# Maxima of attention scores: one whole tile and half of another per window, instead of one and a half shared tiles

## The chip, the cores and the metric

The kernel runs on one core of one Trainium2 chip. The metric is the device time of one execution in microseconds. The kernel before was run three times: 1779.7, 1775.07 and 1778.25 us, median 1778.25 us.

A core has five engines that run side by side and meet only at semaphores: TensorE (matmuls, "PE" in the profile, its weight loads "PEld"), VectorE ("DVE"), ScalarE ("ACT"), GpSimd ("POOL") and SyncE ("SP"), which issues the DMAs here. Matmuls write to PSUM, which has eight banks of 2 KB per partition; 128x512 float32 values fill one bank. VectorE and ScalarE read PSUM and write SBUF.

## The reference, cut to what matters

```
x = x + layernorm(attention(layernorm(x)))
x = x + layernorm(ffn(layernorm(x)))

attention: q = x @ Wq  (16 heads of 16),  k, v = x @ Wk, x @ Wv  (4 heads, each used by 4 query heads)
           q, k = rope(q), rope(k)
           p = softmax(q k^T / sqrt(D))          D = 256
           out = (p v) @ Wo
ffn:       x @ (ternarized weight * alpha)^T + bias
```

The input is 8 sequences of 1024 tokens with 256 features. The softmax needs, for every query and head, the maximum of its scores over all 1024 keys before the exponentials are taken. Float32 accuracy is kept by splitting numbers into a high and a low part and stacking them along the contraction dimension.

## The kernel before, in words

**Units, blocks, windows.** The 8192 tokens form 16 units u of 512 queries (two per sequence). A unit has four blocks, j = 0 to 3, so there are 64 blocks i = 4u + j. A block computes four heads for 512 queries: for each of 8 key tiles kt, four exp tiles of 128 keys x 512 queries, 32 exp tiles in all, numbered s. Four exp tiles are a step; a unit has 32 steps. The work of a block is cut into windows: ten of three exp tiles and one of two (`windows`, L1057). The last twelve steps of the kernel are "late": their windows hold four exp tiles and no maxima.

**Two passes over the scores.** The scores are computed twice. The second pass (`exp_scores`, L659) has keys on the PSUM partitions and queries along the free dimension; ScalarE takes exp of them (L678), and the matmuls "av" (L698) multiply the result by v. The first pass (`max_scores`, L575) has queries on the partitions and keys along the free dimension, so that VectorE can reduce each row to its maximum (L621). It runs about 48 half tiles (a block and a half) ahead of the exps. Each half tile is one matmul over 512 keys; a whole maxima tile covers the 1024 keys in two halves. There are 2048 half tiles, as many as exp tiles.

**Rows of the array.** Both passes contract over 64 rows: for each head half a (0 or 1) the rows 64a to 64a+63 of the stacked queries `q_st` and keys `k_st`. Matmuls on opposite row halves run side by side on TensorE.

**How a window interleaves.** `window` (L1099) issues one exp tile, one maxima half tile, one exp tile and so on, three of each. So a whole maxima tile starts in one window and every second one is finished in the next. A tile "sm" has two PSUM banks, and the pool `ps_mx` holds two such tiles; `ps_e` holds three single banks for exp tiles (and, during the main part, for all projection and tail products, through `psum`, L186); the last bank is for av.

**The tile that crosses a window.** From block 9 on (and except for every eighth block, whose maxima need both halves alone) the crossing tile is treated differently: its first half is computed with key differences `k_df` (second 512 keys minus the first 512), ScalarE takes Relu of it into `rest` (`positive_differences`, L626, at the end of the window, after the three exps), the second half is the scores of the first 512 keys, and one fused VectorE operation adds the two and takes the maximum (L617), since max(s1, s2) = s1 + relu(s2 - s1). There are 245 such tiles. Both halves lie in the same tile "sm", in different banks.

**Maxima to shift rows.** When a block's maxima are all read, `shift_split` (L632) splits them into a high and a low part on VectorE, and two steps later `shift_rows` (L641) transposes them on TensorE ("pm"), copies them on ScalarE ("mh") and issues two DMAs (L654), one for each a, which write them as extra rows of `q_st`. The exp matmuls of that block read these rows. `parts_of_step` (L1076) tests, at the end of every step, whether a transpose is due; a window of three tiles ends a step in three windows out of four.

**Parts.** Between the exps of a window and its av matmuls `parts_of_step` also issues the projection and tail pieces of other units, at steps given by the tables `P_PARTS` and `T_PARTS` (L952 to L971). The av matmuls of a window are those of two windows earlier.

**Order.** The order on TensorE, VectorE and ScalarE is written out by hand (the program order). In the main part GpSimd and the DMA issues on SP are ordered by the framework's scheduler. Every engine works strictly in its order. Whole tiles are tracked for dependences.

**The start.** Before the first exp there are ten steps of maxima alone, four half tiles each (`start_step`, L1082).

Of the kernel before, what the change touches and what calls it, by code (L numbers as in the profile page):

```python
# [8 lines left out]
F32 = mybir.dt.float32  # L9
# [20 lines left out]
def kernel(  # L30
# [49 lines left out]
    avp = ctx.enter_context(tc.tile_pool(name="avp", bufs=5))  # L80
    tailp = ctx.enter_context(tc.tile_pool(name="tailp", bufs=1))
    dram = ctx.enter_context(tc.tile_pool(name="dram", bufs=3, space=DRAM))
    ps_mx = ctx.enter_context(tc.tile_pool(name="ps_mx", bufs=2, space=PSUM))
    ps_e = ctx.enter_context(tc.tile_pool(name="ps_e", bufs=3, space=PSUM))
    ps_av = ctx.enter_context(tc.tile_pool(name="ps_av", bufs=1, space=PSUM))

# [99 lines left out]
    def psum(shape, name, dtype=F32):  # L186
        if spare[0]:
            spare[0] += 1
            if spare[0] % 5 < 2:
                return ps_mx.tile(shape, dtype, tag="sm", name=name)  # L190
        return ps_e.tile(shape, dtype, tag="se", name=name)


# [114 lines left out]
    class Project:  # L308
# [3 lines left out]
        def __init__(self, u, eng):  # L312
            self.u, self.eng = u, eng
            self.b, self.half = divmod(u, UPB)
            self.xt, self.sc, self.hl = {}, {}, {}
            self.q_rot = None
            if u not in (1, 2):
                xn = qkp.tile([P, UT, D], F32, tag="xn", name=f"xn_{u}", bufs=2)
                xs = qkp.tile([P, 2, UT, D], F32R, tag="hl", name=f"xs_{u}")
                self.xn = [xn[:, 2 * p : 2 * p + 2, :] for p in range(2)]  # L320
                self.xs = [[xs[:, l, 2 * p : 2 * p + 2, :] for l in range(2)] for p in range(2)]
            else:
                self.xn = [
                    tailp.tile([P, 2, D], F32, tag=f"xn{p}", name=f"xn_{u}_{p}") for p in range(2)
                ]
                self.xs = [
                    [ep.tile([P, 2, D], F32R, tag="e", name=f"xs_{u}_{p}_{l}") for l in range(2)]
                    for p in range(2)
                ]
# [238 lines left out]
    def block_queries(i, r2=slice(None)):  # L568

        u, j = divmod(i, G)  # L570
        if u < NU - 1:
            return q_st[u % 2][:, j, r2, :]
        return q_st[u % 2][:, :, r2, j * P : (j + 1) * P]

    def max_scores(v, end):  # L575

        i, k = divmod(v // 2, 2 * NK)  # L580
        u, part = i // G, v % 2
        if i == 0:
            a, ch, t, r2 = 1 - part, k // NK, k // 2 % UT, k % 2
        else:
            a, ch, t, r2 = 1 - k % 2, part, k // 4, k // 2 % 2
        queries = block_queries(i, r2)
        queries = queries[:, t * P : (t + 1) * P] if u < NU - 1 else queries[:, t]
        keys = k_st[(u // UPB) % 2][:, :, ch * 512 : (ch + 1) * 512]
        if part == 0:
            sm[0] = ps_mx.tile([P, 2, 512], F32, tag="sm", name=f"sm_{i}_{k}")  # L590
            if k == 0:
                mx[i] = small.tile([P, 2, UT, 2], F32, tag="mx", name=f"mx_{i}")
            if k == 0 and i == 0:
                mx["half"] = small.tile([P, 2, 2, UT, 2], F32, tag="mx0", name="mx_half", bufs=1)
            sm["rest"] = None
            if v + 1 == end and u >= UPB and i % (UPB * G) > 0:
                sm["rest"] = work.tile([P, 512], F32, tag="rest", name=f"rest_{i}_{k}")
                keys = k_df
        elif sm["rest"] is not None:
            keys = k_st[(u // UPB) % 2][:, :, :512]  # L600
        rows = slice(64 * a, 64 * a + 64)
        nc.tensor.matmul(  # L602
            sm[0][:, part, :],
            queries[rows],
            keys[rows, r2],
            start=True,
            stop=True,
        )
        if part == 0:
            return  # L610
        if i == 0:
            nc.vector.tensor_reduce(mx["half"][:, ch, ::-1, t, r2], sm[0], AX.X, ALU.max)
            if k == 2 * NK - 1:
                nc.vector.tensor_tensor(mx[0], mx["half"][:, 0], mx["half"][:, 1], ALU.max)
        elif sm["rest"] is not None:
            rest, m = sm["rest"], mx[i][:, a, t, r2 : r2 + 1]
            nc.vector.tensor_tensor_reduce(  # L617
                rest, sm[0][:, 1, :], rest, 1.0, LEAST, ALU.add, ALU.max, m
            )
        else:  # L620
            nc.vector.tensor_reduce(mx[i][:, a, t, r2 : r2 + 1], sm[0], AX.XY, ALU.max)  # L621
        if k == 2 * NK - 1:
            shift_split(i)
            due.append((v // 4 + (1 if i < 2 else 2), i))

    def positive_differences(v):  # L626
        if v % 2 and sm["rest"] is not None:
            nc.scalar.activation(sm["rest"], sm[0][:, 0, :], AF.Relu)  # L628

    sm, mhl, shifts = {}, {}, {}  # L630

    def shift_split(i):  # L632

        m = mx.pop(i)
        hl = mhl[i] = small.tile([P, 2, 2, 2 * UT], F32R, tag="mhl", name=f"mhl_{i}")
        order = "(r t)" if i // G < NU - 1 else "(t r)"
        hi, lo = (hl[:, :, l].rearrange(f"p a {order} -> p a t r", r=2) for l in range(2))
        nc.vector.tensor_copy(hi, m)  # L638
        split_lo(nc.vector, lo, m, hi)
# [19 lines left out]
    def exp_scores(n, r2, a, sc):  # L659
        i, kt = divmod(n, NK)  # L660
        queries = block_queries(i, r2)
        rows = slice(64 * a, 64 * a + 64)
        nc.tensor.matmul(  # L663
            sc if len(queries.shape) == 2 else sc.rearrange("p (j t) -> p j t", j=G),
            k_st[(i // G // UPB) % 2][rows, r2, kt * P : (kt + 1) * P],
            queries[rows],
            start=True,
            stop=True,
        )

    def exp_one(s):

        n, (a, r2) = s // 4, divmod(s % 4, 2)
        i, kt = divmod(n, NK)
        e = es[n, r2, a] = ep.tile([P, UQ], F32, tag="e", name=f"e_{i}_{kt}_{r2}_{a}")
        sc = ps_e.tile([P, 512], F32, tag="se", name=f"se_{i}_{kt}_{r2}_{a}")
        exp_scores(n, r2, a, sc)
        nc.scalar.activation(e, sc, AF.Exp, scale=1.0 / D**0.5)  # L678

    def exp_two(n, r2):  # L680

        i, kt = divmod(n, NK)
        sc = ps_mx.tile([P, 2, 512], F32, tag="sm", name=f"se_{i}_{kt}_{r2}")
        for a in range(2):
            exp_scores(n, r2, a, sc[:, a, :])
        for a in range(2):
            e = es[n, r2, a] = ep.tile([P, UQ], F32, tag="e", name=f"e_{i}_{kt}_{r2}_{a}")
            nc.scalar.activation(e, sc[:, a, :], AF.Exp, scale=1.0 / D**0.5)

    def av_piece(i, first, end):  # L690

# [30 lines left out]
    class Tail:  # L722
# [9 lines left out]
        def new(self, what, p):  # L732
            shape, dtype = ([P, 2, 2, D], F32R) if what == "hl" else ([P, 2, D], F32)
            return tailp.tile(shape, dtype, tag=f"{what}{p}", name=f"{what}_{self.u}_{p}")
# [7 lines left out]
        def tiles(self, p):  # L742
            return slice(self.width * p, self.width * (p + 1))
# [306 lines left out]
    for k, *p in L_PARTS:  # L1050
        at(SPU * (NU - 1) + k, part, tails, NU - 1, *p)

    def maxima_by(s):

        return s + 4 * START + 2 * sum(s >= k for k in (28, 36, 52, 68))

    def windows():  # L1057


# [11 lines left out]
                yield i, s, size, s >= ends  # L1071
                s += size

    maxima = [0]

    def parts_of_step(n):  # L1076
        if due and due[0][0] <= maxima_by(4 * n + 4) // 4 - 1:
            shift_rows(due.pop(0)[1])
        for f, args in todo.pop(n, ()):
            f(*args)  # L1080

    def start_step(n):  # L1082
        for _ in range(4):
            max_scores(maxima[0], None)
            maxima[0] += 1
        parts_of_step(n)

    behind, done = [], []
# [10 lines left out]
    def window(i, s, size, late):  # L1099
        if done:  # L1100
            av_out(done.pop())
        if late:
            for r2 in range(2):
                exp_two(s // 4, r2)
        else:
            end = min(maxima_by(s + size), 4 * NSTEP)
            for q in range(max(size, end - maxima[0])):
                if q < size:
                    exp_one(s + q)
                if maxima[0] < end:  # L1110
                    max_scores(maxima[0], end)
                    maxima[0] += 1
            positive_differences(maxima[0])
        behind.append((i, s, size))
        for n in range(s // 4, (s + size) // 4):
            parts_of_step(n)
        av_windows(1 if late else 2)
# [59 lines left out]
    with tc.manual_schedule(engines={E.PE, E.DVE, E.Activation}):  # L1177
        for w in work_left:
            window(*w)
        av_windows(0)  # L1180
        av_out(NU * G - 1)
        assert not todo and not due
    spare[0] = 1
    with tc.manual_schedule(engines={E.PE, E.DVE, E.Activation, E.Pool}):
        last = tails[NU - 1]
# [67 lines left out]
```

## Time and profile before

| what | value |
|---|---|
| median of three runs | 1778.25 us |
| profiled execution | 1778.75 us |
| span of the profiled execution | 1777.0 us |
| mean granted TensorE clock | 0.988 |
| TensorE busy | 1635.8 us, 92% of the span |
| ScalarE busy | 1391.9 us, 78% |
| VectorE busy | 1272.2 us, 72% |
| GpSimd busy | 846.1 us, 48% |

The costliest groups, with the mean duration of one instruction:

| line, engine | what | count | mean ns |
|---|---|---|---|
| L678 ACT | exp of a tile of scores, 128x512 | 2000 | 604 |
| L621 DVE | maximum over a whole tile, 128x1024 to 128x1 | 763 | 1219 |
| L612 DVE | the same for block 0, 128x1024 to 128x2 | 16 | 1220 |
| L617 DVE | fused add and maximum, 128x512 | 245 | 692 |
| L628 ACT | Relu of the differences, 128x512 | 245 | 626 |
| L663 PE | scores for exp | 2048 | 434 |
| L602 PE | scores for maxima | 1803 + 245 | 454, 458 |

How to read it. "Busy" counts the time in which an instruction was running; matmuls overlap, so their durations are longer than the distance from one start to the next. The chain of waits follows the execution back from its end: at each instruction to what released it, or to the instruction before it on its engine. A row of the waits view names who waited, for whom, the total in us, how often, and the longest. In the timeline each row is a start, a duration, the engine, the line, and what it writes and reads; a bracket gives the idle time before it and what ended it.

### The profile page before, as it was taken

To read this page: it belongs to the slowest core of one execution; us is meant where nothing else is said; L and a number is where in the kernel's file an instruction comes from. 1 tells how busy PE (TensorE), PEld (TensorE's weight loads), DVE (VectorE), ACT (ScalarE), POOL (GpSimd) and SP (SyncE) were. 2 spreads that over 40 slices of the span, in tenths; PEclk is the share of its full clock that TensorE was granted. 3 is DMA by queue.
4 is the path that set the end of the run, shared out by engine and by line. 5 is a ranking of instruction groups with operands and counts; after the bars stand their busy time and mean duration, and the time that the engine had idled before them with its cause. 6 is when DMAs were issued, how large, how long until landed. Compare 5 with 4: busy or idle time off the path is not lost.

```text
span 1777.0 us, 36663 instructions
## 1 busy us (share of the span) xinstructions
PE 1635.8 (92%) x14200; PEld 843.9 (47%) x14200; DVE 1272.2 (72%) x1997; ACT 1391.9 (78%) x2724; POOL 846.1 (48%) x1259
## 2 busy tenths in 40 slices
PE   7999899989999999999999999999999999999997
PEld 5544354444544445454444445444454444444444
DVE  6777787666776677767777677766777667777764
ACT  4667678788887878878788787888878788888885
POOL 5543374373744536364373745537373452323354
PEclk8899999999999999999999999999999999999999
DMA  4151425142251513315141241513325141231100
GB/s 125 52 102 42 94 67 108 44 91 60 81 97 42 102 46 86 79 58 99 53 99 46 82 93 42 107 46 84 65 62 101 38 97 41 47 68 32 39 13 25
DMA packets 91790, 122.41 MB, mean 69 GB/s; under 512 B 12872, under 2 KB 55176, under 8 KB 91496
## 3 DMA queue, kind: packets, MB, share of 16 engines
q1 hardware_dynamic: 91616, 120.06, 29.2%
q8 instruction: 112, 1.84, 0.5%
q14 instruction: 62, 0.51, 0.1%
HBM read 71.27 MB, written 47.71 MB: 67 GB/s over the span
## 4 chain that ended last, share of the span: by engine, by line
PE 52%; ACT 28%; DVE 8%; POOL 4%; DMA 4%; issue 3%; SPq 1%; ACTq 0%; POOLq 0%
ACT e L678 21%; PE av L698 17%; PE se L663 15%; PE sm L602 9%; ACT rest L628 5%; DVE mx L621 4%; PE pa L286 3%; PE pq L286 2%; PE pf L286 2%; PE pkv L286 1%; ACT avsb L711 1%; PE pt_xt L270 1%; DVE rest L617 1%; PE pt_ot L270 1%; DVE mhl L638 1%
## 5 line engine op out<-in xcount | busy, mean ns | idle before, releaser
L678 ACT ACTIVATE e<-se 128x512 f32<-128x512 f32 x2000 | 1082.1, 604 | 254.6 <-PE sm L602 206.4
L621 DVE TENSOR_REDUCE mx<-sm 128x1 f32<-128x1024 f32 x763 | 916.4, 1219 | 167.7 <-PE sm L602 137.2
L663 PE MATMUL se<-q_st,k_st 64*128 64x512 f32 x2048 | 704.3, 434 | 9.9 <-DMA q_st<-mh 8.8
L602 PE MATMUL sm<-k_st,q_st 64*128 64x512 f32 x1803 | 578.6, 454 | 72.9 <-ACT rest L628 64.8
L698 PE MATMUL av<-e,v_aug 128*32 128x256 f32 (+3 forms) x8096 | 591.4, 392 | 0.0
L663 PEld LDWEIGHTS se<-q_st,k_st 64*128 64x128 f32 x2048 | 342.3, 186 | 378.6 <-ACT e L678 247.0
L617 DVE CUSTOM_DVE_ANT_0 rest<-sm,rest 128x512 f32<-128x512 f32 x245 | 169.5, 692 | 285.9 <-PE sm L602 281.1
L602 PEld LDWEIGHTS sm<-k_st,q_st 64*128 64x128 f32 x1803 | 244.8, 187 | 158.6 <-ACT rest L628 122.0
L698 PEld LDWEIGHTS av<-e,v_aug 128*32 128x32 f32 x8096 | 184.4, 109 | 190.1 <-issue 141.2
L244 POOL TENSOR_SCALAR lnsc<-mv 128x2 f32<-128x2 f32 (+1 forms) x134 | 26.1, 195 | 479.6 <-DVE mv L242 474.7
L628 ACT ACTIVATE rest<-sm 128x512 f32<-128x512 f32 x245 | 153.5, 626 | 0.9 <-PE sm L602 0.9
L602 PE MATMUL sm<-k_df,q_st 64*128 64x512 f32 x245 | 112.2, 458 | 9.2 <-DVE mx L621 7.4
L772 POOL TENSOR_TENSOR xn<-xn,a 128x512 f32<-128x512 f32 x30 | 38.4, 1281 | 139.3 <-DMA a<-d_rec 139.2
L833 POOL TENSOR_TENSOR a<-a,bias_bc 128x512 f32<-128x512 f32 x30 | 39.0, 1301 | 125.6 <-ACT a L832 125.6
L245 POOL TENSOR_TENSOR lnsc<-lnsc,mhalf 128x2 f32<-128x2 f32 (+1 forms) x134 | 92.7, 692 | 0.9
L165 POOL TENSOR_TENSOR hl<-xn,hl 128x512 fp32r<-128x512 f32 x60 | 76.4, 1284 | 0.5
L602 PEld LDWEIGHTS sm<-k_df,q_st 64*128 64x128 f32 x245 | 45.0, 184 | 47.4 <-DVE mx L621 40.2
L256 POOL TENSOR_SCALAR xn<-x,lnsc 128x256 f32<-128x256 f32 x116 | 64.3, 562 | 3.4
L300 POOL TENSOR_TENSOR t<-q_rot,sin_q_sb 128x512 f32<-128x512 f32 x31 | 40.0, 1290 | 15.6 <-ACT q_rot L452 15.6
L240 DVE BATCH_NORM_STATS2 bnst<-a 128x6 f32<-128x256 f32 x120 | 44.6, 413 | 3.7 <-POOL a L833 3.7
L286 PE MATMUL pa<-woh,hl 128*128 128x256 f32 x240 | 46.1, 294 | 0.4 <-ACT e L678 0.2
L240 DVE BATCH_NORM_STATS2 bnst<-x 128x6 f32<-128x256 f32 x124 | 46.0, 413 | 0.7 <-DMA x<-in_L_attn_x 0.7
(168 smaller groups left out, 1469.6 us busy)
## 6 DMA issues: line engine op xcount, KB each, us to landing
q_st<-dq SPq DMA_DIRECT2D x90, 256.0 KB
dq<-hlq SPq DMA_DIRECT2D x60, 256.0 KB
d_av<-avsb SPq DMA_DIRECT2D x60, 256.0 KB
x<-in_L_attn_x SPq DMA_DIRECT2D x15, 512.0 KB
xn<-d_av SPq DMA_DIRECT2D x30, 256.0 KB
a<-d_rec SPq DMA_DIRECT2D x30, 256.0 KB
xr<-in_L_attn_x SPq DMA_DIRECT2D x15, 512.0 KB
out_x<-a SPq DMA_DIRECT2D x30, 256.0 KB
```

Source lines behind the costliest of these rows:

```text
L165: eng.tensor_tensor(lo, src, hi.bitcast(F32), ALU.subtract)
L240: nc.vector.bn_stats(st[:, t, :], src[:, t, :])
L245: nc.gpsimd.tensor_tensor(sc[:, 1, :], sc[:, 1, :], mhalf[:, :n], ALU.pow)
L256: eng.tensor_scalar(dst[:, t, :], src[:, t, :], sc[:, 0, t : t + 1] if eng is nc.gpsimd else mv[:, t, 0:1], sc[:, 1, t : t + 1], ALU.add i ...
L286: nc.tensor.matmul(out, chunk(left[i], c), chunk(right[j], c), start=(k == 0), stop=(k == len(steps) - 1),)
L602: nc.tensor.matmul(sm[0][:, part, :], queries[rows], keys[rows, r2], start=True, stop=True,)
L617: nc.vector.tensor_tensor_reduce(rest, sm[0][:, 1, :], rest, 1.0, LEAST, ALU.add, ALU.max, m)
L621: nc.vector.tensor_reduce(mx[i][:, a, t, r2 : r2 + 1], sm[0], AX.XY, ALU.max)
L628: nc.scalar.activation(sm["rest"], sm[0][:, 0, :], AF.Relu)
L663: nc.tensor.matmul(sc if len(queries.shape) == 2 else sc.rearrange("p (j t) -> p j t", j=G), k_st[(i // G // UPB) % 2][rows, r2, kt * P : ...
L678: nc.scalar.activation(e, sc, AF.Exp, scale=1.0 / D**0.5)
L698: nc.tensor.matmul(av_ps[0][32 * r : 32 * r + 32, lo:hi], va[:, kt, r, :], es[i * NK + kt, r // 2, r % 2][:, lo:hi], start=(kt == 0 and lo ...
```

## The change

The crossing tile disappears. A window of three now holds one whole tile (two matmuls, one head half a) and one half of another. The pool `ps_mx` keeps its four banks, but as one tile "two" of two banks and a ring of two single banks "one". The whole tile goes through tag "two" with a single buffer, each half through tag "one". Late windows and spare tiles use the same tags.

Halves always belong to head half 0. First and second halves alternate from window to window; where differences apply, the first half is the one with `k_df` and the Relu, the second the one with the fused operation, as before. In the other blocks (block 0 to 8 and then every eighth) each half is reduced by itself, every reduction writes one maximum per half, and `shift_split` takes the larger of the two. Whole tiles belong to the head half opposite to the window's last exp tile, and the order of heads among the four exp tiles of a key tile now follows a pattern of three. The first exp tile of a block is now one of head half 1. The reads are issued after all matmuls of the window: the whole tile's reduction first, then the half's Relu, fused operation or reduction.

A shift transpose is due 8 half tiles after its block's maxima are read (4 for blocks 0 and 1), counted in half tiles issued. Four places in the first blocks (`AHEAD`) issue two more half tiles each, which brings the lead to 48. The two-exp window of a block holds a whole tile and no half.

```diff
-    ps_mx = ctx.enter_context(tc.tile_pool(name="ps_mx", bufs=2, space=PSUM))
+    ps_mx = ctx.enter_context(tc.tile_pool(name="ps_mx", bufs=1, space=PSUM))
...
+        def whole(self, a):
+            i, halves = self.next_tile(a)
+            tile = ps_mx.tile([P, 2, 512], F32, tag="two", name=f"sm_{i}_{a}_{halves[0][1]}")
+            self.done += 2
...
+        def half(self):
+            first = self.open is None
+            if first:
+                self.open = (*self.next_tile(0), None)
+            i, halves, rest = self.open
...
+            tile = ps_mx.tile([P, 512], F32, tag="one", name=f"sh_{i}_{t}_{r2}_{ch}", bufs=2)
+            self.done += 1
...
+                if not self.differences(i):
+                    m = mx[i][:, ch, 0, t, r2 : r2 + 1]
+                    nc.vector.tensor_reduce(m, tile, AX.X, ALU.max)
+                elif first:
+                    nc.scalar.activation(rest, tile, AF.Relu)
+                else:
+                    m = mx[i][:, 0, t, r2 : r2 + 1]
+                    nc.vector.tensor_tensor_reduce(
+                        rest, tile, rest, 1.0, LEAST, ALU.add, ALU.max, m
+                    )
...
+        def read(self, i):
+            self.unread[i] -= 1
+            if self.unread[i] == 0:
+                shift_split(i)
+                due.append((self.done + (4 if i < 2 else 8), i))
...
+    def exp_order(s):
+        kt = s // 4 % NK
+        if s < 4 * NK and kt >= 2:
+            kt -= 2
+        a = ((1, 0, 0, 1), (0, 0, 1, 1), (1, 1, 0, 0))[kt % 3]
+        q = s % 4
+        return a[q], a[:q].count(a[q])
...
     def parts_of_step(n):
-        if due and due[0][0] <= maxima_by(4 * n + 4) // 4 - 1:
+        if due and due[0][0] <= maxima.done + behind_maxima[0]:
             shift_rows(due.pop(0)[1])
...
+            work, reads = [], []
+            if size == 3 or maxima.done + 1 == 4 * NSTEP:
+                work, read = maxima.half()
+                reads.append(read)
+            if size > 1:
+                two, read = maxima.whole(1 - exp_order(s + size - 1)[0])
+                work += two
+                reads.insert(0, read)
+            for q in range(size):
+                exp_one(s + q)
+                if q < len(work):
+                    work[q]()
+            for read in reads:
+                read()
```

## The prediction

> **What bounds the kernel now.** Read the page's chain of waits first, because engine shares mislead here: TensorE is 92% busy, yet its part of the chain is 52%.
>
> ```profile
> PE 52%; ACT 28%; DVE 8%; POOL 4%; DMA 4%; issue 3%; SPq 1%; ACTq 0%; POOLq 0%
> ACT e L678 21%; PE av L698 17%; PE se L663 15%; PE sm L602 9%; ACT rest L628 5%; DVE mx L621 4%; PE pa L286 3%; PE pq L286 2%; PE pf L286 2%; PE pkv L286 1%; ACT avsb L711 1%; PE pt_xt L270 1%; DVE rest L617 1%; PE pt_ot L270 1%; DVE mhl L638 1%
> ```
>
> The chain alternates between TensorE and ScalarE, so a dependence between them sets the pace. Who waits for whom names it:
>
> ```profile
> PEld sm L602 <- ACT rest L628: 122.0, 183, 0.8
> PE sm L602 <- ACT rest L628: 64.8, 178, 0.5
> PE sm L602 <- DVE mx L621: 13.9, 35, 1.3
> PE se L663 <- DMA q_st<-mh: 8.8, 5, 5.4
> ```
>
> Columns: total us, times, longest. The second half of a shared maxima tile is not written until the Relu has read the first half, although they lie in different banks. The timeline shows two windows (block 8) and this wait:
>
> ```profile
> 283.20 1.58 ACT L678 ACTIVATE e<-se 128x512 f32<-128x512 f32 x3 [0.47 <-PE sm L602]
> 283.23 0.39 PE L602 MATMUL sm<-k_df,q_st 64*128 64x512 f32 x1
> 283.46 1.22 DVE L621 TENSOR_REDUCE mx<-sm 128x1 f32<-128x1024 f32 x1 [0.49 <-PE sm L602]
> 283.56 0.86 PE L698 MATMUL av<-e,v_aug 128*32 128x128 f32 x16
> 284.35 0.49 PE L663 MATMUL se<-q_st,k_st 64*128 64x512 f32 x1
> 284.65 0.62 ACT L628 ACTIVATE rest<-sm 128x512 f32<-128x512 f32 x1
> 285.12 0.63 ACT L678 ACTIVATE e<-se 128x512 f32<-128x512 f32 x1
> 285.32 0.50 PE L602 MATMUL sm<-k_st,q_st 64*128 64x512 f32 x2 [0.48 <-ACT rest L628]
> 286.21 0.64 PE L698 MATMUL av<-e,v_aug 128*32 128x256 f32 x8
> ```
>
> The window starting at 282.66 takes 1.68 us. The next starts at 284.35 with one exp matmul, then stands until 285.32, because the Relu started at 284.65 after three exps: 2.43 us. The pair takes 4.11.
>
> TensorE's own window, from the same starts: pairs of matmuls in opposite row halves at 0, 0.335 and 0.57, the av matmuls 0.32 after the third pair, the next window 0.785 later: 1.675 us. The Relu's loop costs 0.75 a pair.
>
> **The change, part by part.** *Matmuls:* 2048 exp, 2048 maxima and the av matmuls remain. Within a window the new order of heads still puts opposite row halves next to each other: e1 h0 | e0 w1 | e0 w1, or e1 h0 | e1 w0 | e1 w0. Nothing gained or lost.
>
> *Removed:* the wait for the Relu, since each half now has its own bank and its ring of two is read long before reuse.
>
> *Added:* the only whole tile ("two", one buffer) cannot be written before VectorE has read the last window's. From rows: second matmul of the tile to start of the reduction 0.46 (283.00 to 283.46); reduction 1.225; its end to the released matmul 0.054 (in each such wait); after that standstill the tile's second matmul comes 0.335 later (460.68 to 461.02). Loop: 0.46+1.225+0.054+0.335 = 2.08 us. TensorE alone goes from one tile to the next in 0.32+0.785+0.335 = 1.44, against 1.74: it stands 0.30 and restarts 0.10 slower. Behind the waiting matmul stand, in program order, the window's third exp matmul, its parts and the av matmuls; ScalarE waits for the exp. So a plain pair goes from 4.11 to 4.16: **the loop through ScalarE is exchanged for one through VectorE of the same length.**
>
> The gain is in windows that carry projection or tail matmuls: these stand between the tile's end and the next tile and cover the reduction. Such a window costs 1.675 plus its part: 0.51 (four transposes), 1.15 (eight matmuls) or 1.62 (twelve). In the kernel before the part comes on top of the Relu's wait in every second window.
>
> Here a rule speaks against the change. The Trainium skill, "Perfetto Trace Analysis", section Optimizing Tensor Performance, says that independent matmul groups should rotate through different PSUM banks so that one's evacuation overlaps the next's matmuls; one whole tile doesn't rotate. If nothing covered it, each of some 640 windows would pay 1.74 instead of 0.40, +860 us. The row decides: exp, half and av matmuls use other banks and cover 1.44 of it. I take 0.40.
>
> *ScalarE* keeps its exps and 245 Relus (640 halves in windows make as many split tiles). Seven activations a pair at 0.477 from start to start are 3.34 of 4.16: not the bound. A part's PSUM tile waits for the first exp of its window, as now: 0.29 where the window before had a part too, and 0.2 in each block's third window, which starts with the avsb copy.
>
> *VectorE:* in the 15 blocks without differences, some 160 single-bank reductions replace 80 double ones. No row shows one: between 610 ns (half of 1219) and 692 (the fused op on 512). By the latter it adds 80 x (2x692-1219) = 13 us, beside TensorE; I take nothing on the path, at most 13. Layer-norm statistics (0.96 a batch) delay the next reduction: after a window with a fused op, 0.46+1.14+0.62+0.96 = 3.18 against 2.08+0.46, so 0.66, once in a j=0 block; elsewhere they follow a window with a part.
>
> *Moved:* the shift rows. A block's maxima are complete in its sixth window, as before, but the transpose pm (due 8 halves later, tested only where a step ends) goes from the eighth to the tenth window, two of 2.08 later. Then mh is copied and SP issues two DMAs. Rows: issues 0.72 apart; landing to first exp 2.13 after issue (361.24 to 363.37 below). In addition the first exp is now head half 1, which needs the second DMA. From the tenth window's last maxima matmul: pm at 0.32, ScalarE free for mh at 1.02, first issue 1.29, second 2.01, usable 4.14. The next block's first exp would start at 2.08+0.32+0.785 = 3.18 plus the eleventh window's part. With no part (j=0) it is late by 0.96, of which 0.56 counts, since the standstill for the reduction lies in it. Parts of 1.15 and 1.62 leave 0.2 and 0.7 us spare. SP's queue is the danger; its timeline at the end of block 10:
>
> ```profile
> 356.90 4.30 SPq L493 DMA_DIRECT2D k_st<-dk  x6
> 361.24 1.41 SPq L654 DMA_DIRECT2D q_st<-mh  x2
> 362.75 2.34 SPq L437 DMA_DIRECT2D dkd<-dkds  x4
> ```
>
> In j=2 blocks of odd units the shift DMAs stood behind the key stacking, whose dk comes from POOL and DRAM: issued 25.1 to 26.4 us into the block in four of them, 24.7 and 24.1 in two. The block gets shorter, the DMA chain doesn't: by the sum below the landing is 0.2 to 2.7 late, 1.6 on average, where now it is just in time. If SP orders them otherwise this goes to nothing; if they fall behind the next four DMAs (2.34 us), to 5.
>
> **The sum,** by blocks of 32 exps (ten windows of three, one of two, four kinds j=0 to 3), against starts read from the trace (282.66, 306.71, 334.86, 363.37, 391.00):
>
> - j=0: 8x2.08 + (2.19+0.2) + (2.19+0.29) + 2.19 + 0.66 + 0.56 = 24.9; now 24.0. 14 blocks: +12.
> - j=1: 7x2.08 + 2.19 + (3.30+0.29) + (2.19+0.29) + 3.30 = 26.1; now 28.0 in eleven, 26.6 to 28.5 in three. -24.
> - j=2: 8x2.08 + (3.30+0.2) + 3.30 + 3.30 = 26.7; now 26.4 in five even units; 27.5 to 28.8 in six odd ones, +1.6 for the landing there. +2.
> - j=3: 5x2.08 + 3x2.19 + (2.19+0.29+0.2) + (2.83+0.29) + 2.83 = 25.6; now 27.6 in six, 26.3 in the five that hold no Relu for most of the block, 26.8 and 27.7 in two. -18.
> - Start and the first eight blocks: no Relu there to save, VectorE on the chain (its pairs of reductions take 2.37); between -5 and +15, taken as +5 (DMA landings and single reductions).
> - The last twelve steps and the last tail: same banks, same instructions, 0.
>
> Sum -23 against the profiled span of 1777.0, that is 1754.0, or 1755.75 with the 1.75 that lies around the span (run 1778.75). The runs' median is 1778.25, 0.5 below; from it: **1755 us.**
>
> **Rivals.** (1) *The full exchange:* shift rows land in time everywhere and statistics find cover, so 14x(0.56+0.66) + 10 of late landings go: 1755-27 = 1728. For it: SP often idles for over ten us. Against: four odd units have no slack now.
>
> (2) *Nothing gained:* parts' gains are eaten by VectorE, if half of the other seven batches of statistics per unit pay 0.44 more: 15x7x0.5x0.44 = +23, 1778. Against: they come after windows with large parts.
>
> (3) *Slower:* the shift DMAs, now last before use, get queued behind other SP work. Place: first exp of every block. Price: one more group of 1.6 us (three q_st<-dq and a fill) before them makes the four transitions late by 1.6, 0.9, 0.9 and 1.4 more (1.6 less the spares of 0.7, 0.7, 0.2): 4.8 a unit, x14 = 67 us, giving 1822; at the units' ends and the odd units alone (14x1.4 + 6x1.6 + 14x0.56) some +37, 1792. It decides from a mean of 0.4 us per block (23 us over 56 blocks). For it: SP is the one queue not ordered by hand, and the next unit's queries come free in the tenth window. Against: before, those DMAs came after the shift rows.
>
> (4) *The change doesn't do what it says:* TensorE still waits for the Relu through another dependence: 0.75 on top of some of the 2.08 loops. The halves are separate tiles; little chance, and it would be slower too.
>
> **How the numbers follow.** Forecast 0.47 (own range 1740 to 1771), full exchange 0.13, nothing gained 0.12, SP queue 0.25, Relu still waited for 0.03. Some 5 us (0.3%) is what a measurement tells from none. Faster: 0.45 of the forecast's 0.47 and all of (1), 0.58; same: 0.02 and 0.08 of (2), 0.10; the rest, with 0.04 of (2), slower, 0.32. The range leaves out 0.1 at each end: 1726 to 1800.
>
> **What would show it.** Right: TensorE's wait for ACT rest is gone; sm waits for DVE mx some 400 times; plain windows start 2.08 apart; windows with twelve matmuls take about 3.3 to 3.6; se waits for q_st<-mh at some twenty block starts, up to 2.7 us. Wrong: q_st<-mh waits at most block starts, plain windows far from 2.08, or gaps at the reduction beyond 0.7 in many windows.

## The result: 5% slower, and the profile after

The changed kernel takes 1865.56 us (median of four runs, 1864.16 to 1867.1) beside 1776.66 us for the kernel before (now a median of four runs). The ratio is 1.0499, with a 95% interval of 1.048 to 1.0517. The experiments below have their own runs of the kernel before beside them (medians 1778.51 to 1780.23 us), and their ratios are to these. One run of `due3` took 2260.02 us at a granted clock of 0.698 and is left out of its median. The profiled execution has a span of 1863.6 us at a mean granted TensorE clock of 0.957; before it was 1777.0 us at 0.988.

The chain of waits of the kernel after, by engine and by line:

```profile
PE 54%; ACT 12%; DMA 12%; DVE 11%; POOL 6%; SPq 3%; issue 2%; POOLq 0%; ACTq 0%; DVEq 0%
PE av L772 17%; PE se L719 14%; PE sm L620 11%; ACT e L747 9%; DMA q_st<-mh 7%; DVE mx L637 5%; PE pa L286 3%; PE pkv L286 2%; SPq L710 1%; PE pt_xt L270 1%; ACT rest L672 1%; DMA k_rot<-d_k 1%; DVE mx L642 1%; PE pq L286 1%; DVE bnst L240 1%
```

ScalarE's share has fallen from 28% to 12%, as it should when the Relu's loop goes. DMA has tripled, from 4% to 12%, and 7% of the chain is q_st<-mh alone: the shift rows. TensorE's longest waits in the kernel after (total us, times, longest us):

```profile
PE se L719 <- DMA q_st<-mh: 115.8, 40, 7.3
PE sm L620 <- DVE mx L637: 7.7, 19, 0.9
```

The 64.8 us for the Relu are gone. In their place stands what was fourth with 8.8 us: the first exp of a block waits for its shift rows. The plain windows do what was forecast. TensorE's timeline in block 12, the first exp of four windows and one wait for the whole tile:

```profile
431.82 0.50 PE L719 MATMUL se<-q_st,k_st 64*128 64x512 f32 x1
...
433.49 0.50 PE L719 MATMUL se<-q_st,k_st 64*128 64x512 f32 x1
...
435.58 0.50 PE L719 MATMUL se<-q_st,k_st 64*128 64x512 f32 x1
...
437.63 0.50 PE L719 MATMUL se<-q_st,k_st 64*128 64x512 f32 x1
...
438.78 0.49 PE L620 MATMUL sm<-k_st,q_st 64*128 64x512 f32 x1 [0.42 <-DVE mx L637]
```

The distances are 1.67, 2.09 and 2.05 us: a plain window behind a plain one settles at the 2.08 worked out from the reduction's loop, after a first one that finds the tile free.

### The profile page after: what moved, and what is told of

The parts are those of the page before. It is cut to its first block, busy times and chain, and to the rows that moved or that the text cites. A ratio compares the mean times of both kernels' runs of the same rounds, so it can differ in the third digit from the quotient of the medians.

```text
span 1863.6 us, 36435 instructions
## 1 busy us (share of the span) xinstructions
PE 1679.1 (90%) x14200; PEld 836.1 (45%) x14200; DVE 1281.3 (69%) x2091; ACT 1374.8 (74%) x2724; POOL 845.2 (45%) x1259
## 3 DMA queue, kind: packets, MB, share of 16 engines
q8 instruction: 112, 1.84, 0.4%
## 4 chain that ended last, share of the span: by engine, by line
PE 54%; ACT 12%; DMA 12%; DVE 11%; POOL 6%; SPq 3%; issue 2%; POOLq 0%; ACTq 0%; DVEq 0%
PE av L772 17%; PE se L719 14%; PE sm L620 11%; ACT e L747 9%; DMA q_st<-mh 7%; DVE mx L637 5%; PE pa L286 3%; PE pkv L286 2%; SPq L710 1%; PE pt_xt L270 1%; ACT rest L672 1%; DMA k_rot<-d_k 1%; DVE mx L642 1%; PE pq L286 1%; DVE bnst L240 1%
## 5 line engine op out<-in xcount | busy, mean ns | idle before, releaser
L637 DVE TENSOR_REDUCE mx<-sm 128x1 f32<-128x1024 f32 x539 | 659.1, 1223 | 445.6 <-PE se L719 247.8
L719 PE MATMUL se<-q_st,k_st 64*128 64x512 f32 x2048 | 759.9, 465 | 115.8 <-DMA q_st<-mh 115.8
L620 PE MATMUL sm<-k_st,q_st 64*128 64x512 f32 x1398 | 504.9, 440 | 16.7 <-DVE mx L637 7.7
L244 POOL TENSOR_SCALAR lnsc<-mv 128x2 f32<-128x2 f32 (+1 forms) x134 | 25.6, 191 | 552.3 <-DVE mv L242 547.4
L642 DVE TENSOR_REDUCE mx<-sm 128x2 f32<-128x1024 f32 x160 | 195.8, 1224 | 92.5 <-PE sm L620 47.8
L620 PE MATMUL sh<-k_st,q_st 64*128 64x512 f32 x405 | 209.7, 521 | 4.3 <-DVE mx L670 4.0
L675 DVE CUSTOM_DVE_ANT_0 rest<-sh,rest 128x512 f32<-128x512 f32 x245 | 166.6, 680 | 0.1
L672 ACT ACTIVATE rest<-sh 128x512 f32<-128x512 f32 x245 | 155.1, 633 | 0.0
L620 PE MATMUL sh<-k_df,q_st 64*128 64x512 f32 x245 | 126.0, 514 | 0.0
L670 DVE TENSOR_REDUCE mx<-sh 128x1 f32<-128x512 f32 x160 | 107.8, 680 | 0.0
L620 PEld LDWEIGHTS sh<-k_st,q_st 64*128 64x128 f32 x405 | 77.6, 193 | 10.1 <-DVE mx L670 8.2
```

Of the source, the lines that this page charges most:

```text
L620: nc.tensor.matmul(dst, queries[rows], keys[rows, r2], start=True, stop=True)
L637: nc.vector.tensor_reduce(mx[i][:, a, t, r2 : r2 + 1], tile, AX.XY, ALU.max)
L642: nc.vector.tensor_reduce(dst, tile, AX.X, ALU.max)
L670: nc.vector.tensor_reduce(m, tile, AX.X, ALU.max)
L672: nc.scalar.activation(rest, tile, AF.Relu)
L675: nc.vector.tensor_tensor_reduce(rest, tile, rest, 1.0, LEAST, ALU.add, ALU.max, m)
```

## The experiments

**Theory:** the new windows gain what the sum says, and the loss comes from the shift rows alone: the transpose pm, two windows later, makes them land after TensorE is ready. **Rivals:** the new windows themselves are slow; or the granted clock is the cause and not a consequence.

### Moving the transpose alone, in both kernels

`due6` is the kernel after with the transpose due two half tiles earlier, which puts pm back in the eighth window. `before_late` is the kernel before with pm moved to the tenth. `due3` moves pm to the seventh window.

```diff
-                due.append((self.done + (4 if i < 2 else 8), i))
+                due.append((self.done + (4 if i < 2 else 6), i))
```

> The changed kernel with the shift transpose due 6 instead of 8 half tiles after a block's maxima, which puts it back into the eighth window (the tenth in the changed kernel). Theory L (the shift rows land too late, and TensorE then runs at half clock for a while): the wait of se for q_st<-mh falls from 115.8 us to under 20, the granted clock returns to 0.98 or more, and the time is 1725 to 1750 us, faster than before. Rival V (the single whole tile and its loop through VectorE is what costs): the waits fall, but the time stays above 1800 us.

```diff
-            due.append((v // 4 + (1 if i < 2 else 2), i))
+            due.append((v // 4 + (1 if i < 2 else 3), i))
```

> The kernel before with the shift transpose one step later, which puts it into the tenth window of a block; nothing else of the change. Theory L: most of the loss appears here without the change, se waits 70 to 110 us for q_st<-mh, the clock falls to about 0.96, 1830 to 1880 us. Rival V: within 10 us of 1777.

`due3` differs from `due6` only in its 3 in place of 6.

> As due6, but the transpose due 3 half tiles after the maxima, so in the seventh window. Theory L: no wait is left that earliness can remove (what remains stands in SP's queue behind the key stacking), within 6 us of due6 (1749). If lateness still costs in due6: 8 us or more below it.

Measured: `due6` 1749.32 us, ratio 0.9834 (0.9802 to 0.9866); `before_late` 1875.05, ratio 1.0537 (1.0484 to 1.0589); `due3` 1747.19, ratio 0.9816 (0.9794 to 0.9839). TensorE's wait for the shift rows in `due6`:

```profile
PE se L719 <- DMA q_st<-mh: 10.0, 5, 5.5
```

and TensorE's two longest waits in `before_late`:

```profile
PE se L663 <- DMA q_st<-mh: 100.2, 39, 5.3
PE sm L602 <- ACT rest L628: 51.9, 154, 0.5
```

The late transpose makes the old kernel some 97 us slower, and without it the new one is 29 us faster than the old (both beside 1778.51). So the windows are not slow. The place of one small transpose decides the sign. One window earlier still, in `due3`, adds nothing that the runs can tell: 2 us, with runs of one kernel up to 7 us apart. In the eighth window it is early enough.

### Which part of the late landing costs what

The landing isn't late for one reason. In the kernel after, from block 8 on, the waits at the starts of blocks are of three kinds: 3.1 to 3.9 us at the start of a unit (2 to 14), 1.9 to 2.3 us after a unit's first block (units 2 to 10, then 0.5 to 0.9), and 5.0 to 7.3 us ahead of the fourth block of every second unit (2 to 12). Elsewhere there is none, but for two of 0.8 near the end.

The first kind, the start of unit 3. The kernel after, the chain of waits in order of time (start us, us, what):

```profile
411.74 0.09 ACT mh L703
411.83 0.02 issue
411.84 0.67 SPq L710
412.51 0.04 issue
412.56 5.05 DMA q_st<-mh
417.61 0.14 issue
417.75 0.47 PE se L719
```

and its SP queue there, in the timeline:

```profile
410.55 0.78 SPq L559 DMA_DIRECT2D q_st<-dq  x2
411.84 1.37 SPq L710 DMA_DIRECT2D q_st<-mh  x2
413.25 1.91 SPq L559 DMA_DIRECT2D q_st<-dq  x4
```

mh ends at 411.83 and the DMA is issued at 411.84, so SP isn't late at all. The transfer of 8 KB takes 5.05 us because it runs among six 256 KB stackings (two issued ahead of it, four behind) of the next unit's queries.

The third kind, block 11. The kernel after, SP's timeline:

```profile
375.35 3.83 SPq L493 DMA_DIRECT2D k_st<-dk  x6
379.22 1.09 SPq L437 DMA_DIRECT2D dkd<-dkds  x2
382.47 0.78 SPq L493 DMA_DIRECT2D k_df<-dkd  x2
383.35 1.09 SPq L437 DMA_DIRECT2D dkd<-dkds  x2
384.54 1.40 SPq L710 DMA_DIRECT2D q_st<-mh  x2
```

Here mh was ready at 376.6. SP issues it at 384.54: the scheduler has put the writes and first reads of the key differences ahead, and SP stands from 380.3 to 382.5 until a write has landed. The transfer itself is then as short as in the prediction, 1.97 us in the chain.

Four kernels separate the first and the third. `a1first` issues the DMA that the first exp needs ahead of the other one. `actq` issues both on ScalarE's queue, so that they no longer stand in SP's order. `shift_first` holds the stacking of the next queries behind the shift DMAs of the block concerned. `shift_first2` holds the writes of the key differences behind theirs as well.

```diff
-        for a in range(2):
+        for a in (1, 0):
```

> The changed kernel with the shift DMA of head half 1, which the first exp needs, issued ahead of that of head half 0 (0.72 us from issue to issue). Theory L: each of some 40 waits gets up to 0.7 us shorter, 1830 to 1850 us. Rival O (the loss is the order of heads, whose first exp needs the second DMA): the waits go and the time is under 1790.

```diff
-            shifts[i] = nc.sync.dma_start(out=dst, in_=mh[n * a : n * a + n, :]).ins
+            shifts[i] = nc.scalar.dma_start(out=dst, in_=mh[n * a : n * a + n, :]).ins
```

> The changed kernel with the two shift DMAs issued on ScalarE's queue instead of SP's. If the SP queue's order is what delays them: the 5 to 7 us waits in the third block of odd units fall to about 1, the 3 to 4 us waits between units stay where the transfer itself is slow (5.05 us instead of 2.0 beside the next unit's queries), 1810 to 1840 us. If it is the lateness alone whatever the queue: waits of odd units stay, within 10 us of 1865.

```diff
-        at(SPU * (u - 1) + 1, stack_queries, u)
+        at(SPU * (u - 1) + 1, behind_shift, G * (u - 1), stack_queries, u)
```

> The changed kernel, with the next unit's query DMAs (q_st<-dq, six of 256 KB) held back until the shift DMAs of the block that starts have been issued. If the shift transfer is slow because it shares the DMA engines with them (5.05 us instead of 2.0 between units): the waits of 3.1 to 3.9 us at the start of each unit fall under 0.7, the others stay, 1805 to 1825 us. If those waits are the lateness of the transpose alone: they stay, 1855 us or more.

```diff
-            for l in range(2):
-                for e in range(2):
-                    nc.sync.dma_start(out=dst[l, e], in_=hl[:, l, e, :].bitcast(F32))
+            def issue():
+                for l in range(2):
+                    for e in range(2):
+                        nc.sync.dma_start(out=dst[l, e], in_=hl[:, l, e, :].bitcast(F32))
+
+            if tag == "dkd" and self.u > 3:
+                behind_shift(G * (self.u - 2) - 1, issue)
+            else:
+                issue()
```

> The kernel of the run that put the stacking of the next queries behind the shift DMAs, and now the four writes dkd<-dkds of the key differences are held behind the shift DMAs of the block in question too, so that these stand on SP right behind the key stacking and before the writes and the reads k_df<-dkd that wait for them. Theory (the 5 to 8 us at the fourth block of every second unit are SP's queue: the shift rows stand behind writes and reads of the key differences): these six waits fall to 1 to 3 us, those after the first blocks of units (about 2.3 us) stay, TensorE waits for q_st<-mh some 40 to 50 us instead of 75, and the time falls from 1814 to 1780 to 1797. Rival (the key stacking alone, which comes late from POOL and DRAM, holds the queue): the waits stay above 4 us and the time within 6 us of 1814. Whatever is left over the 1749 of the kernel with the earlier transpose is then the transpose's own place and the transfers beside which it runs.

| kernel | us, median | ratio to before (95%) | wait for shift rows, us (times) | unit starts | after first blocks | fourth block of every second unit |
|---|---|---|---|---|---|---|
| after | 1865.56 | 1.0499 (1.048 to 1.0517) | 115.8 (40) | 3.1 to 3.9 | 1.9 to 2.3 | 5.0 to 7.3 |
| a1first | 1858.10 | 1.0443 (1.0409 to 1.0477) | 101.5 (44) | 2.4 to 3.3 | 1.7 to 2.1 | 4.8 to 7.6 |
| actq | 1923.15 | 1.0813 (1.0775 to 1.085) | 164.9 (40) | 8.8 to 10.0 | 2.1 to 2.5 | 0.9 to 3.2 |
| shift_first | 1814.05 | 1.0187 (1.0165 to 1.0209) | 75.4 (26) | 0 | 1.9 to 2.8 | 5.0 to 7.9 |
| shift_first2 | 1772.33 | 0.9948 (0.9933 to 0.9962) | 43.5 (23) | 0 | 1.8 to 2.7 | 0 to 2.8 |
| due6 | 1749.32 | 0.9834 (0.9802 to 0.9866) | 10.0 (5) | 0 | 0 | 0 to 1.7 |

The last three columns are the lengths of single waits in us, for the units just named (units 2 to 10 for the second kind).

`a1first` gained 7 us where 15 and more were expected, a miss. Where the shift transfer is alone, in the last three units, the wait did fall by the issue distance, from 0.8 or 0.9 us to 0.2. At unit starts it fell by 0.6 on average, after first blocks (units 2 to 10) by 0.2, at the fourth blocks not at all. And of the 14 us less waiting half came back: the first two windows of blocks 8 to 61 take 7.4 us more, at a mean clock of 0.952.

`actq` is the larger miss, and the more telling one. Its chain at a unit's start:

```profile
418.37 0.27 ACT mh L703
418.64 0.02 issue
418.66 0.65 ACTq L710
419.31 0.04 issue
419.35 11.57 DMA q_st<-mh
430.92 0.14 issue
431.06 0.76 PE se L719
```

The DMA is issued at once on its own queue, and it takes 11.57 us, with three of the stackings put in motion by SP at 417.37, ahead of it, and three more at 419.42, while it runs. A queue of its own did not help this transfer beside the large ones. The Trainium skill ("DMA: Bandwidth & Descriptors", section Issuing engines are not separate DMA queues) says that DMAs of all issuing engines run on the same 16 DMA engines and interleave there. At the fourth blocks, where SP's order was the cause, the same edit took the waits from 5.0 to 7.3 down to 0.9 to 3.2. What is left there is not SP's order: in all six, ScalarE issues the DMA 1.7 to 4.1 us after mh is ready, released by the landing of a key stacking (k_st<-dk).

In `shift_first` the waits at unit starts go to nothing (51 us less), in `shift_first2` those at the fourth blocks shrink too (42 us less). The first came in where the theory put it; the second is 8 us below the range given, with its waits as expected. In `shift_first2`, the same stretch of SP's timeline:

```profile
371.61 3.53 SPq L499 DMA_DIRECT2D k_st<-dk  x6
375.18 1.41 SPq L716 DMA_DIRECT2D q_st<-mh  x2
376.69 2.34 SPq L438 DMA_DIRECT2D dkd<-dkds  x4
```

The shift rows stand right behind the key stacking, as they do in `due6`. With pm still in the tenth window, order on SP alone turns 5% slower into 0.5% faster. What is left to `due6`, 23 us, lies where blocks begin: over blocks 8 to 61 the last windows, in which the waits fall, hold 15.7 us more, and the first two 7.3.

### What a standstill costs beyond itself

In block 11 of the kernel after the wait is not over when the rows land. Busy time of PE, PEld, DVE, ACT and POOL by stretch, then the granted clock, DMA share and GB/s:

```profile
380.00:387.30 7.30, 0.13 (x4) 0.00 (x0) 0.00 (x0) 0.00 (x0) 7.14 (x10) 0.82 0.22 60
387.30:388.00 0.70, 0.62 (x4) 0.58 (x6) 0.00 (x0) 0.00 (x0) 0.70 (x2) 0.50 0.35 82
...
390.00:391.00 1.00, 1.00 (x12) 0.50 (x6) 0.33 (x1) 0.25 (x1) 1.00 (x3) 0.50 0.27 100
391.00:392.00 1.00, 0.88 (x7) 0.38 (x3) 0.08 (x1) 0.77 (x2) 1.00 (x2) 0.75 0.00 0
392.00:394.00 2.00, 1.95 (x18) 1.04 (x18) 1.75 (x3) 2.00 (x5) 2.00 (x2) 1.00 0.00 0
```

TensorE comes back at half clock and has it until about 391.5; its first window takes 3.02 us instead of 1.68. To price this, `warm_wait` adds matmuls of its own ahead of the first exp of a block, into that exp's PSUM tile, which the exp then overwrites: 22 of them at the fourth blocks, 12 at unit starts, 6 after first blocks.

```diff
+        if s % (4 * NK) == 0 and 8 <= s // (4 * NK) < 62:
+            j = s // (4 * NK) % (2 * G)
+            for _ in range({0: 12, 4: 12, 1: 6, 5: 6, 3: 22}.get(j, 0)):
+                nc.tensor.matmul(sc, ident_r, k_st[n // NK // G // UPB % 2][:, 0, :512], start=True, stop=True)
```

> The changed kernel with dummy matmuls of 128x512 written into the PSUM tile of a block's first exp, where TensorE waits for the shift rows anyway (12 at the start of a unit, 6 at its second block, 22 at the fourth block of every second unit[...]). If the half clock after a wait comes from TensorE standing idle: windows 0 and 1 of the blocks lose some 24 us in sum, the granted clock returns to 0.98, 1835 to 1850 us, with the same waits for the DMA. If the clock falls for another reason: within 6 us of 1865.

Measured: 1851.83 us, ratio 1.0398 (1.0374 to 1.0421), 2 us above what was expected, and a mean clock of 0.984 instead of 0.957. TensorE at the start of block 11:

```profile
376.30 5.40 PE L744 MATMUL se<-k_st,ident_r 128*128 128x512 f32 x22
382.05 0.50 PE L719 MATMUL se<-q_st,k_st 64*128 64x512 f32 x1 [0.35 <-DMA q_st<-mh]
```

The rows still land late (5.75 us after the added matmuls begin, against a stop of 7.25), but the exp now runs at full clock (0.50 us against 0.76). Over blocks 8 to 61 the first two windows of all blocks get shorter by 27.8 us in sum, while the last windows, with the added matmuls, take 8.6 us more and the windows between 5.5 more. Half clock is a consequence of the waits and costs time of its own. Of the 111 us that lie between the kernel after and `due6` in these blocks, the first two windows hold 24.

### A version that beats both

`due6` still pays the single whole tile: 2.05 in a plain window behind a plain one. `split_ring` puts every half tile into a bank of its own, one ring of four; a whole tile is then two single-bank reductions, and the Relu or fused operation is issued right behind the window's first pair. The maxima are kept per half in all blocks.

```diff
-            tile = ps_mx.tile([P, 2, 512], F32, tag="two", name=f"sm_{i}_{a}_{halves[0][1]}")
+            tiles = [
+                ps_mx.tile([P, 512], F32, tag="one", name=f"sm_{i}_{a}_{h}_{self.done}", bufs=4)
+                for h in range(2)
+            ]
...
-                due.append((self.done + (4 if i < 2 else 8), i))
+                due.append((self.done + (4 if i < 2 else 6), i))
...
+                if q == 0 and early:
+                    early[0]()
```

> As due6, but every maxima half tile has a bank of its own in one ring of four; a whole tile is two single-bank reductions (0.60 us from start to start instead of 1.14 for both at once), and the Relu or the fused operation of the half is issued ahead of the rest. If the loop through VectorE (single whole tile) is what holds plain windows at 2.05 us: they fall to 1.7 to 1.8 and the time to 1665 to 1700 us. If VectorE itself becomes the bound: 1730 to 1760 us.

Measured: 1702.44 us (1697.6 to 1704.15), ratio 0.9553 (0.9531 to 0.9574), 2 us above the range of the theory that the single whole tile was the bound, and far from its rival's 1730 to 1760. Half of the plain windows take 1.70 us or less (1.86 in `due6`), a quarter still 2.18 or more. Page of `split_ring`, the cost of it on VectorE:

```profile
PE 1589.0 (93%) x14200; PEld 785.8 (46%) x14200; DVE 1365.9 (80%) x2888; ACT 1367.9 (80%) x2724; POOL 848.2 (50%) x1259
...
L639 DVE TENSOR_REDUCE mx<-sm 128x1 f32<-128x512 f32 x1398 | 892.6, 683 | 134.7 <-PE se L716 95.4
```

Two reductions of 683 ns replace one of 1223, so VectorE has 83 us more to do than in `due6` (1282.7), and the kernel is 47 us faster all the same: VectorE's load was not the bound. The ring and the earlier reads were not tried apart.

## Why the prediction was wrong

**Right: the windows.** The wait for the Relu is gone. Ahead of a whole tile TensorE (PE and PEld together) waits for the reduction 407 times (some 400 forecast). Plain windows behind plain ones settle at 2.05 to 2.09 us (2.08 forecast). Without its landing terms, 14 x 0.56 and 6 x 1.6, the sum over the blocks was -45 us (12 - 24 + 2 - 18, less 17.4); `due6` has -40.8 over blocks 8 to 61. By kind of block the mean lengths in `due6` are 23.4, 26.7, 26.3 and 26.1 us, against 24.3 (24.9 less the 0.56), 26.1, 26.7 and 25.6 forecast. The start and the first eight blocks were taken as +5; `due6` has +12.7, inside the -5 to +15.

The kinds miss by up to 0.9 us in both directions, so that the total, 4 us off, is closer than its parts: in that much it is luck. One placement in the sum is wrong without harm. A part stands behind its own window's tile, so it covers the reduction for the next window, not for its own. In `due6` a three-exp window with twelve matmuls takes at least 3.64 us, loop and part (2.05 + 1.62), where the sum had 3.3 to 3.6, and the plain window behind a part takes 1.69 on average, where it had 2.08. Each part covers one reduction either way.

**Wrong: the landing, under "Moved".** Some twenty waits for the shift rows, of at most 2.7 us, were forecast; there were 40, of up to 7.3. The prediction priced the landing at 2.13 us from issue to first exp everywhere, and from that concluded that "parts of 1.15 and 1.62 leave 0.2 and 0.7 us spare". It took that duration from a place where the transfer ran alone. Where it runs alone in the kernel after, the waits are 0.5 after the first blocks of units 11 and 12 and 0.8 to 0.9 in the last three units, against 0.96 worked out, of which 0.56 was counted. Everywhere else something is beside it:

- At unit starts the spare of 0.2 became a wait of 3.1 to 3.9, because the transfer takes about 5 us among the six stackings. In the kernel before the stackings were issued 4.4 us after the shift rows (387.72 against 383.35); the prediction had seen that and counted it only as queueing, in rival 3.
- After first blocks the 0.56 became about 2. During that wait the DMA engines are 62% busy with 205 GB/s. In the chain at block 13 SP issues the DMA 0.47 us after mh is ready, behind an input load, and the transfer takes 3.03 us instead of 1.97; the two make up the difference. What stretches the transfer there was not tried by itself.
- At the fourth blocks of every second unit 1.6 became 5.0 to 7.3. mh is ready 3.9 us later relative to the point where TensorE stands, and the scheduler lets the writes of the key differences go first, which makes the issue 5.9 us later than in `due6`. The prediction had a late order on SP as its end of 5 and took 1.6. (It spoke of odd units: these blocks belong to even units from 2 to 12, whose projected unit is odd.)

**Missing: the clock.** No term of the sum stood for the granted clock after a standstill. The Trainium skill has the rule ("TensorE: Matmul & The Clock Gate", Part 1): the clock falls to half after at least one idle window of about 3.4 us. The runs show the fall, and at shorter stops too (last section). With landings taken as 0.56 and 1.6 us it had no place in the sum; with waits of 3 to 7 us it has, for some 24 to 28 us.

**The sum, corrected.** Between the kernel before and after, the starts of their last windows lie 86.4 us apart: -40.8 from the windows as in `due6`, +111.4 that `due6` takes away again (last windows of blocks, where the waits stand, +88.2; first two windows, mostly half clock, +24.4; the rest -1), +17.2 in the start and the first eight blocks, and -1.4 in the end.

**The rivals.** Rival 3 was the case that came: SP's order and the transfers, with the place (every first exp) and the sign right. Its price, one more group of DMAs of 1.6 us, gave 1822 at most. It failed as the forecast did: it moved the issue and left the transfer at its length. Its argument against itself, that the stackings came after the shift rows before, is the one that the later transpose undoes. Rivals 1 and 2 describe what `due6` lies between (1749, against 1728 and 1778), and rival 4 fell with the Relu's wait.

## What to carry to other kernels

When a small transfer is moved later, its issue and duration must be read again at the new place, from what else is in flight there; a duration measured alone is the floor. Ask of every DMA beside it whether an order outside the program will now put it in front. Where a transfer sits just before its use, pull its producer forward first: two windows were worth 116 us here.

## What the runs showed of the hardware that was not expected

An 8 KB transfer took 1.97 us with the DMA engines 17% busy (block 11), 5.05 us with two of six 256 KB transfers issued ahead of it on its own queue and four behind, and 11.57 us from another queue with three issued ahead and three right after.

The half clock comes in stretches of about 3.4 us, and not always at the stop. In block 11 of the kernel after, a mean of 0.82 over 7.3 us means 2.6 us at half, so from 384.7, and then to 391.5: 6.8 us. In `shift_first2` TensorE stood only 1.84 us at the same place, came back at full clock, and fell to half 1.3 us later (the same columns):

```profile
376.20:378.00 1.80, 0.00 (x0) 0.03 (x1) 0.00 (x0) 0.00 (x0) 1.80 (x4) 1.00 0.06 15
378.00:379.00 1.00, 1.00 (x10) 0.63 (x14) 0.00 (x0) 0.50 (x2) 1.00 (x2) 1.00 0.28 76
379.00:380.00 1.00, 1.00 (x18) 0.30 (x17) 0.96 (x1) 1.00 (x4) 1.00 (x2) 0.66 0.28 82
380.00:381.00 1.00, 1.00 (x10) 0.90 (x6) 0.26 (x1) 0.76 (x3) 1.00 (x2) 0.50 0.29 84
381.00:382.00 1.00, 1.00 (x8) 0.45 (x4) 0.31 (x1) 1.00 (x3) 1.00 (x1) 0.50 0.05 15
382.00:383.00 1.00, 1.00 (x11) 0.31 (x9) 1.00 (x2) 0.92 (x2) 0.84 (x4) 0.63 0.53 78
```

From 0.66 and 0.63 in the two slices at its ends, half clock lasted from 379.3 to 382.7. A wait of 2.10 us in block 13 of the kernel after brought none. So a stop well under 3.4 us can cost half clock, and not each does.

The clock records say more. In every trace but that of `due3`, all changes of the clock lie on one grid of 3.413 us (in the kernel after, for instance, at 384.68, 391.51, 418.81 and 422.23). The stop of 1.84 us fell whole into one interval of the grid (375.92 to 379.33), and the next interval was at half. That of 2.10 us was cut by a boundary at 442.70 into 0.36 and 1.74, and neither was followed by half clock. So where a stop lies on the grid matters, besides its length. No sharp limit comes out: 1.82 us of standing in one interval left the clock full (`before_late`, from 517.8), 1.38 us brought half (`split_ring`, from 826.2). What decides between them stays open, and no kernel here moved a stop along the grid.
